# Shifted rows in two transfers, scores kept with negative sign, and other orders at the passages of a two-block kernel

## The chip, the cores and the metric

The kernel runs as one program on one core of one Trainium2 chip. The metric is the device time of one execution in microseconds (us). Before the change three runs took 1590.53 to 1592.78 us, with a median of 1591.86 us.

The core's engines each work through their own instructions in the order in which the program gives them: PE (matrix products and transposes), DVE (vector work), ACT (activations), POOL (further vector work) and SP, which here only issues transfers (DMA). Engines wait for each other through semaphores.

## The reference

The input `x` has two batches of 2048 tokens of 256 numbers. Two blocks follow, each added back to its input after a layer norm. The first block is an attention in three branches (compressed, selected, windows); the change doesn't touch it. The second has two layers of local attention and gated units, and the change lies there. Cut to that:

```python
def shift_token(t):
    t1, t2 = jnp.split(t, 2, axis=-1)
    t2 = jnp.pad(t2, ((0, 0), (1, 0), (0, 0)))[:, :-1]
    return jnp.concatenate([t1, t2], axis=-1)

def _layer(x, wqkv, qs, ksc, wo, lg, lb, w1, b1, w2, b2):
    h = shift_token(x)
    q, k, v = jnp.split(h @ wqkv, 3, axis=-1)       # 8 heads of 64
    q, k = rotary_xpos(l2norm(q) * qs, l2norm(k) * ksc)
    o = local_attention(q, k, v)                    # blocks of 128, one block back, softmax
    x = x + o @ wo
    h = shift_token(x)
    h = (h - h.mean(-1)) / jnp.sqrt(h.var(-1) + 1e-05) * lg + lb
    a, g = jnp.split(h @ w1 + b1, 2, axis=-1)       # 682 wide each
    return x + (a * jax.nn.gelu(g, approximate=False)) @ w2 + b2
```

The second half of a token's numbers thus comes from the token before it. In the attention, a query sees at most 128 keys back; other scores are masked before the softmax.

## The kernel before

**Tiles and stages.** All of `x` stays on chip: `Y[g]` holds a group of four tiles of 128 tokens, with a token's place in its tile as the partition. Groups 0 to 3 (G0 to G3) are batch 0, G4 to G7 batch 1. Up to about 240 us the first block runs (its order is the list FIRST). Then come attention of layer 0, its gated units, attention of layer 1, its gated units.

**How the order is made.** In the second block every step is a small function. `put(place, f, ...)` (line 939) files it under a place in a plan, and at the end (lines 1403 to 1405) all steps are called in order of place; each engine gets its instructions in that order. For the attention the places are those of PLACES (line 950), 12400 apart from one tile to the next (`TILE`). For the gated units they are made by `gated_units` (line 1221), one chunk every 5170 (`STEP`).

**The passages.** Where attention ends and gated units begin, and where gated units of layer 0 end and attention of layer 1 begins, steps of both are mixed. There `in_order` (line 1388) takes all steps of the stretch and puts them in the order of a list of numbers: TO_GATED (line 81, about 300 steps, used in both layers) and TO_ATTENTION (line 93, 204 steps, used once). A number is a step's rank in the plan; `w0` and `w1` are loads of later weights.

**A tile of attention.** `turn_input` transposes the tile on PE, `late_half` and `early_half` copy it to SBUF on ACT, `edge` sets the column that comes from the tile before. `project` makes queries, keys and values on PE; `square`, `sums`, `clip`, `power` and `unit` normalize on ACT, DVE and POOL; `times` and `add` rotate on DVE and POOL; `turn`, `keys` and `queries` bring queries and keys into place. `scores` multiplies them on PE. `tops` (line 1108) adds the mask to the scores with `tensor_tensor_reduce` on DVE, which also returns each row's maximum; a small DVE instruction negates the four maxima of a group of four score blocks into `off`. `exps` (line 1127) takes the exponentials on ACT with `off` as bias, `divide` divides by their sum on DVE, `turn_probs`, `probs` and `weigh` multiply with the values, `sum_first` and `sum_both` bring the result into the tile `oT`, `project_out` and `residual` add it to `Y`.

**A group of gated units.** `shift` (line 1224) makes a tile `sh`: the second halves of the group's rows, one partition further down. For that SP issues transfers: one row from the group before (`kept`), three rows from partition 127 to partition 0, and 127 rows from partitions 0 to 126 to 1 to 127. `moments` (statistics, DVE, from `Y` and `sh`), `deviations` (POOL), `normed` (DVE, eight pieces of a group) and `turned` (transposes on PE, scaling on DVE) make the input of the products. `inner` makes one chunk of gate and value on PE, `gate` does the gelu on ACT and the product on DVE (into `u`), `back` and `back_rest` multiply with `w2` on PE, `back_add` adds to `Y` on DVE, `second_bias` adds `b2` on POOL.

**Buffers.** `sh` and `oT` share one tag with two buffers. The banks of PSUM are three tags: `pa` and `pb` with two banks each, `pc` with four.

**Scores of the first block.** `win_score` (line 784) already keeps its masked scores with negative sign: scale -1, a minimum, and an exponential with scale -1.

Of the kernel before, what the change touches and what calls it, by code (L numbers as in the profile page):

```python
# [10 lines left out]
F32 = mybir.dt.float32  # L11
I32 = mybir.dt.int32
AF = mybir.ActivationFunctionType
ALU = mybir.AluOpType
AX = mybir.AxisListType

P = 128
B, L, H = 2, 2048, 256
# [18 lines left out]
FMIN = -3.4028234663852886e38  # L37
# [41 lines left out]


TO_GATED = """
39 42 140 0 1 9 18 20 22 2 5 8 11 3 17 7 4 19 24 29 47 41 14 12 15 6 13 16 10 30 33 23 40 21 26 25 34 32 36 48
38 43 54 57 51 46 67 69 35 56 61 70 89 83 64 28 31 58 71 27 45 44 50 53 37 52 63 74 77 55 87 92 59 60 66 90 76
68 73 78 91 49 97 75 62 65 85 98 79 82 84 93 96 119 72 81 80 109 123 122 101 99 103 86 121 135 94 102 120 112
118 125 127 107 126 131 129 134 113 116 115 128 88 100 105 95 110 106 114 117 104 108 139 144 111 136 143 137
150 180 167 124 133 145 149 151 141 147 158 159 132 138 155 183 185 166 170 174 152 162 165 169 130 148 142 156
160 153 161 176 146 154 164 171 173 179 178 177 184 157 191 163 172 175 186 189 198 190 194 188 195 168 w0 181
196 204 213 207 211 182 197 202 192 200 205 193 199 201 208 216 220 215 222 210 214 218 203 206 228 187 219 221
226 232 227 229 209 225 231 212 230 223 236 233 234 238 251 242 244 255 217 224 245 246 277 278 235 240 254 272
273 257 263 264 262 249 241 266 261 259 258 260 252 248 267 250 243 268 256 237 239 271 276 247 253 265 279 280  # L90
281 282 286 290 291 297 296 292 298 299 283 287 284 288 293 294 269 285 270 289 295 274 w1 275
"""
TO_ATTENTION = """
45 47 125 128 3 4 9 23 0 1 2 5 6 7 8 15 19 10 12 24 18 16 25 26 29 28 17 11 13 14 22 20 21 27 30 31 38 32 33 36
39 37 34 35 40 46 42 41 43 44 52 53 50 55 48 49 54 56 51 78 57 59 60 63 68 64 58 62 66 61 67 70 72 74 75 94 65
69 80 71 73 77 79 76 84 85 88 92 87 89 96 81 82 83 86 90 91 93 101 98 102 95 97 100 104 106 110 103 107 99 112
133 105 108 111 109 117 113 115 114 118 116 124 119 127 121 122 123 126 132 129 136 130 131 135 140 120 134 139
142 138 137 141 146 144 143 156 w0 147 145 151 150 148 149 152 153 158 154 155 160 159 157 162 165 161 166 164
163 168 172 169 167 171 174 177 181 175 173 170 182 178 183 180 179 184 185 186 191 193 187 190 189 188 195 192
200 196 202 176 201 198 199 194 197  # L100
"""


# [73 lines left out]
def sandwich_kernel(ctx: ExitStack, tc: tile.TileContext, x, Wq, bq, Wk, bk, Wv, bv, Wo, bo, Wg, bg,  # L177
                    Wc, bc, Ws, bs, wqkv, q_scale, k_scale, wo, ln_g, ln_b, w1, b1, w2, b2, rope, out):
    nc = Notes(tc.nc)
# [5 lines left out]
    small = ctx.enter_context(tc.tile_pool(name="small", bufs=6))  # L185
# [781 lines left out]
    def attention(l, base):  # L967
# [107 lines left out]
        def seen(n, half):  # L1075

            return (P - half * HALF if ORDER[n][0] == 0 else 0), KEYS
# [30 lines left out]
        def tops(n, quad):  # L1108

            s = S[n]  # L1110
            s["e", quad] = p = act.tile([P, 2, 2, KEYS], F32, tag="prob", name="prob")
            top = small.tile([P, 4], F32, tag="top4", name="top4")
            s["off", quad] = small.tile([P, 4], F32, tag="off4", name="off4")
            s["den", quad] = small.tile([P, 4], F32, tag="den4", name="den4")
            if ORDER[n][0] == 0:
                for half in range(2):
                    nc.gpsimd.memset(p[:, :, half, 0 : seen(n, half)[0]], 0.0)
            for i in range(2):
                for half in range(2):
                    lo, hi = seen(n, half)  # L1120
                    nc.vector.tensor_tensor_reduce(
                        out=p[:, i, half, lo:hi], in0=s["s", quad][half][:, i, lo:hi], in1=mask_loc[:, lo:hi],
                        scale=1.0, scalar=FMIN, op0=ALU.add, op1=ALU.max,
                        accum_out=top[:, 2 * i + half : 2 * i + half + 1])
            nc.vector.tensor_scalar_mul(s["off", quad], top, -1.0)

        def exps(n, pair):
            s = S[n]
            quad, i = divmod(pair, 2)
            for half in range(2):  # L1130
                lo, hi = seen(n, half)
                ph = s["e", quad][:, i, half, lo:hi]
                j = 2 * i + half
                nc.scalar.activation(ph, ph, AF.Exp, bias=s["off", quad][:, j : j + 1],
                                     accum_out=s["den", quad][:, j : j + 1])

        def divide(n, quad):
# [83 lines left out]
    def gated_units(l, base, no_gate_until, beside):  # L1221
        G = {g: dict(u=U[i % 2]) for i, g in enumerate(GORDER)}

        def shift(g):

            s, y = G[g], Y[g]
            sh = act.tile([P, GT, P], F32, tag="oT", name="sh")
            if g % NG:
                nc.sync.dma_start(sh[0:1, 0, :], G[g - 1]["kept"][P - 1 : P, :])
            else:  # L1230
                nc.gpsimd.memset(sh[0:1, 0, :], 0.0)
            nc.sync.dma_start(sh[0:1, 1:GT, :], y[P - 1 : P, 0 : GT - 1, P:H])
            nc.sync.dma_start(sh[1:P, :, :], y[0 : P - 1, :, P:H])
            s["kept"] = act.tile([P, P], F32, tag="kept", name="kept", bufs=3)
            nc.gpsimd.tensor_copy(s["kept"], y[:, GT - 1, P:H])
            s["sh"] = sh
# [94 lines left out]

        plan = []
        plan += [(-9, shift), (-6, deviations), (-2.5, second_bias), (-2.1, turned, 0), (-1.1, turned, 1)]
        plan += [(-7 + 0.22 * k, moments, k) for k in range(GT)]
        plan += [(-4.5 + 0.22 * (h * GT + k), normed, h, k) for h in range(2) for k in range(GT)]
# [117 lines left out]
```

## Time and profile before

The profiled execution took 1592.03 us; its span from the first to the last instruction is 1590.3 us.

| what | us |
|---|---|
| median of three runs | 1591.86 |
| profiled execution, and its span | 1592.03, 1590.3 |
| PE busy | 1507.6 (95% of the span) |
| DVE busy | 1068.6 (67%) |
| ACT busy | 758.3 (48%) |
| POOL busy | 739.2 (46%) |
| DVE waiting for the shifted rows `sh`, all places | 33.4 |
| ACT waiting for the negated maxima `off`, all places | 19.1 |

Stretches of the span, in us from its start: attention of layer 0 from about 240, the passage to gated units about 590 to 705, gated units to 880, the passage to attention of layer 1 about 880 to 970, attention to 1258, the second passage to gated units to 1370, and gated units to the end.

How to read the views. The page gives sums for the whole span. The table of stretches gives for each the busy time of PE, of PE's weight loads, of DVE, ACT and POOL, with instruction counts in brackets, and then the granted clock of PE as a share of full speed, the busy share of the DMA engines and GB/s. The chain of waits follows the work that ended last back from instruction to instruction: start, duration, what. The timeline lists instructions by start and duration, with the idle time ahead of one in square brackets and what ended it. The groups give engine, operation, output and inputs, shapes, count, then total busy us and mean ns of one, then idle time ahead. L147 is a helper through which all steps of the second block pass and L173 one for the first block, so groups are told apart by their tiles. Matrix products are pipelined, and their ends are modelled.

### The profile page before, as it was taken

The numbers are of one execution on the slowest core, as the hardware profiler recorded it, in microseconds if no ns is written. First come the engines' busy times: TensorE is split into PE (matmuls) and PEld (weight loads), VectorE is DVE, ScalarE is ACT, GpSimd is POOL, SyncE is SP. The second block draws the span as 40 slices with busy tenths as digits, with TensorE's granted clock in tenths as the row PEclk, the third lists the DMA queues.
The fourth block names the chain that finished last, engine by engine and source line by source line (L and its number), as shares of the span: only waits on it lengthen the run. The fifth ranks groups of instructions, "written<-read, shape, count | busy, mean of one in ns | idle before, by whom it ended". The sixth has DMA issues, their size and how long they took to land.

```text
span 1590.3 us, 32477 instructions
## 1 busy us (share of the span) xinstructions
PE 1507.6 (95%) x12344; PEld 983.0 (62%) x12344; DVE 1068.6 (67%) x3139; ACT 758.3 (48%) x2213; POOL 739.2 (46%) x906
## 2 busy tenths in 40 slices
PE   7999958999999999969999999999999989699998
PEld 6877743666666666535555566666666655455554
DVE  6588775787888888634445268888788885255453
ACT  4236564677677676511111157767767764011110
POOL 7214256766666666210111166666666662033233
PEclk9999979999999999989999999999999999899999
DMA  7000001100000000101000020000000000010000
GB/s 223 1 4 5 1 18 37 33 8 6 8 5 9 5 5 8 51 7 27 12 19 0 1 63 7 9 5 9 8 5 8 3 10 6 9 31 28 25 25 30
DMA packets 32510, 30.76 MB, mean 19 GB/s; under 512 B 5154, under 2 KB 30692, under 8 KB 32356
## 3 DMA queue, kind: packets, MB, share of 16 engines
q1 hardware_dynamic: 32164, 28.17, 5.9%
q8 instruction: 98, 1.61, 0.4%
q0 software_dynamic: 192, 0.52, 0.2%
q14 instruction: 56, 0.46, 0.1%
HBM read 20.30 MB, written 4.19 MB: 15 GB/s over the span
## 4 chain that ended last, share of the span: by engine, by line
PE 74%; DVE 3%; DMA 2%; POOL 2%; ACT 1%; issue 1%; SPq 0%; POOLq 0%; DVEq 0%; ACTq 0%
PE pa L147 28%; PE pb L147 24%; PE pc L147 22%; DMA sh<-Y 2%; DVE rr L147 1%; POOL rr L147 1%; DVE prob L147 1%; POOL ss L147 1%; DVE hh L147 0%; DVE Y L147 0%; ACT prob L147 0%; DVE ss L147 0%; ACT probT L147 0%; DVE u L147 0%; ACT sq L147 0%
## 5 line engine op out<-in xcount | busy, mean ns | idle before, releaser
L147 PE MATMUL pa<-wqkv,h 128*128 128x512 f32 x768 | 370.7, 606 | 15.2 <-ACT h L147 11.3
L147 POOL TENSOR_TENSOR rr<-rr 128x256 f32<-128x256 f32 x256 | 184.1, 750 | 308.0 <-DVE rr L147 252.3
L147 ACT ACTIVATE ge<-pa,vb 128x512 f32<-128x512 f32 (+1 forms) x107 | 66.7, 625 | 392.4 <-PE pa L147 324.7
L147 ACT ACTIVATE prob<-prob,off 128x192 f32<-128x192 f32 (+2 forms) x512 | 224.9, 442 | 19.7 <-DVE off L147 19.1
L147 PEld LDWEIGHTS pa<-wqkv,h 128*128 128x128 f32 x768 | 132.3, 191 | 129.1 <-issue 104.7
L147 POOL TENSOR_TENSOR ss<-ss,mhalf 128x16 f32<-128x16 f32 x64 | 187.2, 2925 | 0.8 <-DVE ss L147 0.2
L147 ACT COPY probT<-pb 128x384 f32<-128x384 f32 (+1 forms) x256 | 119.2, 469 | 120.6 <-PE pb L147 117.5
L147 PE MATMUL pa<-hh,w 128*128 128x512 f32 x368 | 171.6, 594 | 0.0
L147 PE MATMUL pb<-hh,w 128*128 128x512 f32 x292 | 141.0, 606 | 26.6 <-DVE u L147 26.6
L147 DVE CUSTOM_DVE_ANT_0 prob<-pc,mask_loc 128x192 f32<-128x192 f32 (+2 forms) x512 | 148.7, 345 | 26.0 <-PE pc L147 20.2
L147 DVE TENSOR_TENSOR rr<-pa,cs 128x1024 f32<-128x1024 f32 x128 | 151.3, 1215 | 21.5 <-ACT sq L147 19.3
L147 PE MATMUL pc<-w,u 128*128 128x256 f32 (+1 forms) x896 | 165.1, 384 | 0.0
L147 DVE SCALAR_TENSOR_TENSOR u<-pb,vb,ge 128x512 f32<-128x512 f32 x73 | 54.6, 750 | 162.3 <-PE pb L147 154.3
L147 PEld LDWEIGHTS pc<-w,u 128*128 128x128 f32 (+1 forms) x896 | 129.7, 174 | 49.0 <-issue 33.8
L147 POOL TENSOR_TENSOR rr<-rr,ss 128x512 f32<-128x512 f32 x128 | 133.1, 1059 | 2.8
L147 DVE TENSOR_TENSOR prob<-prob,den 128x768 f32<-128x768 f32 x128 | 128.1, 1001 | 4.9
L147 POOL TENSOR_SCALAR r<-mv 128x1 f32<-128x1 f32 (+1 forms) x48 | 9.2, 191 | 260.3 <-DVE mv L147 257.8
L147 PEld LDWEIGHTS pb<-ident,prob 128*128 128x128 f32 x752 | 87.9, 141 | 61.0 <-issue 31.1
L147 PE MATMUL pb<-ident,prob 128*128 128x128 f32 x752 | 118.2, 278 | 5.1 <-DVE prob L147 4.1
L147 ACT ACTIVATE sq<-pa 128x512 f32<-128x512 f32 x128 | 75.5, 592 | 98.5 <-PE pa L147 94.0
L147 PE MATMUL pb<-wo,oT 128*128 128x256 f32 x512 | 121.4, 380 | 0.2 <-DVE ss L147 0.2
L147 PEld LDWEIGHTS pb<-hh,w 128*128 128x128 f32 x292 | 56.3, 194 | 98.2 <-issue 69.5
(255 smaller groups left out, 2535.6 us busy)
## 6 DMA issues: line engine op xcount, KB each, us to landing
cs<-in_rope_dram SPq DMA_DIRECT2D x32, 128.0 KB
out_dram<-res SPq DMA_DIRECT2D x32, 128.0 KB
sh<-Y SPq DMA_DIRECT2D x16, 254.0 KB
w<-in_L_ffn_w_dram SPq DMA_DIRECT2D x6, 640.0 KB
X<-_attn_hidden_states_dram SPq DMA_DIRECT2D x7, 512.0 KB
wqkv<-in_L_ffn_wqkv_dram SPq DMA_DIRECT2D x2, 1536.0 KB
Wc<-in_L_attn_Wc_dram SPq DMA_DIRECT2D x1, 1024.0 KB
wo<-in_L_ffn_wo_dram SPq DMA_DIRECT2D x2, 512.0 KB
```

The costliest lines, as they stand in the source:

```text
L147: return f(*a, **k)
```

## The change

Three things change. The step lists TO_GATED and TO_ATTENTION hold the same steps in other orders. In `tops` the score with its mask is multiplied by -1 and its minimum is taken, so that the reduction itself gives `off`; the tile `top` and the negation go, and `exps` gets scale -1. In `shift` the transfer of 127 rows becomes two, of 112 rows (to partitions 16 to 127) and of 15 rows (to partitions 1 to 15).

```diff
@@ tops
             s["e", quad] = p = act.tile([P, 2, 2, KEYS], F32, tag="prob", name="prob")
-            top = small.tile([P, 4], F32, tag="top4", name="top4")
-            s["off", quad] = small.tile([P, 4], F32, tag="off4", name="off4")
+
+            s["off", quad] = top = small.tile([P, 4], F32, tag="top4", name="top4")
...
                     nc.vector.tensor_tensor_reduce(
                         out=p[:, i, half, lo:hi], in0=s["s", quad][half][:, i, lo:hi], in1=mask_loc[:, lo:hi],
-                        scale=1.0, scalar=FMIN, op0=ALU.add, op1=ALU.max,
+                        scale=-1.0, scalar=-FMIN, op0=ALU.add, op1=ALU.min,
                         accum_out=top[:, 2 * i + half : 2 * i + half + 1])
-            nc.vector.tensor_scalar_mul(s["off", quad], top, -1.0)
@@ exps
-                nc.scalar.activation(ph, ph, AF.Exp, bias=s["off", quad][:, j : j + 1],
+                nc.scalar.activation(ph, ph, AF.Exp, bias=s["off", quad][:, j : j + 1], scale=-1.0,
                                      accum_out=s["den", quad][:, j : j + 1])
@@ shift
             nc.sync.dma_start(sh[0:1, 1:GT, :], y[P - 1 : P, 0 : GT - 1, P:H])
-            nc.sync.dma_start(sh[1:P, :, :], y[0 : P - 1, :, P:H])
+
+            for lo, hi in ((16, P), (1, 16)):
+                nc.sync.dma_start(sh[lo:hi, :, :], y[lo - 1 : hi - 1, :, P:H])
```

The lists themselves are long; their parts that matter below, by step (a number after a tile step is the tile, counted 0 to 31 with batches alternating):

| stretch of TO_GATED in layer 0 | before | after |
|---|---|---|
| ahead of shift G4 | project_out 27 is called 35 places before it | project_out 27 is called 31 places before it, at place 197 of the list instead of 141 |
| from shift G4 to its first statistics | 36 other steps | none |
| around the end of tile 31 | probs 31 0, two normed of G4, weigh 31 | probs 31 1, turned G4 1, inner G4 1, gate G0 1, sum_both 30, probs 31 0, weigh 31 |
| around shift G1 | project_out 30, residual 30, shift G1, statistics and normed of G1, inner G4 0 to 2 with gates G4 0 to 2, sum_first 31, back G0 0 to 2, project_out 31 | inner G4 0 to 2 with gates, project_out 30, inner G0 2, gate G0 2, back G0 0 to 2, project_out 31, shift G1, statistics and normed of G1 |
| load of the next layer's wqkv | ahead of values 31 | behind shift G1 |

Behind the list both kernels go on alike: inner G4 3, gate G4 3, back G0 3, shift G5, back_rest G0, turned G1 0, inner G4 4. In TO_ATTENTION the products `back` of G3 move from ahead of the first steps of tile 0 to between them, and the load of a table (table_load 6) moves some 30 places forward.

## The prediction

> **What bounds the kernel now.** I read the page first: PE is busy 95% of a span of 1590.3 us, DVE 67%, the others under half. Only PE's idle time can be gained, so I then cut the span at the passages and read PE busy against the length of each stretch (second and third column):
>
> ```profile
> 330.00:590.00 260.00, 260.00 (x3062) 176.73 (x3053) 213.55 (x576) 182.09 (x577) 169.10 (x177) 1.00 0.02 7
> 590.00:690.00 100.00, 94.54 (x970) 58.79 (x962) 69.08 (x203) 54.64 (x164) 45.41 (x46) 1.00 0.08 25
> 690.00:705.00 15.00, 0.65 (x2) 0.33 (x2) 7.13 (x20) 0.29 (x1) 3.83 (x4) 0.66 0.03 7
> 880.00:970.00 90.00, 88.64 (x512) 52.25 (x514) 48.10 (x126) 38.15 (x116) 44.00 (x53) 1.00 0.10 29
> 1258.00:1357.00 99.00, 93.42 (x961) 58.27 (x959) 67.95 (x199) 53.67 (x160) 45.20 (x45) 1.00 0.03 8
> 1357.00:1370.00 13.00, 0.76 (x3) 0.30 (x2) 5.07 (x20) 0.26 (x1) 1.46 (x3) 0.63 0.04 9
> ```
>
> In steady attention (330 to 590) PE never idles; nothing there can gain. The passage from attention to gated units is idle 5.46 + 14.35 us in layer 0 and 5.58 + 12.24 in layer 1; the passage back (880 to 970) 1.36. The chain of waits names what fills the two long holes, and the timeline shows how:
>
> ```profile
> 680.15 16.07 DMA sh<-Y
> ...
> 1347.24 16.04 DMA sh<-Y
> ```
>
> ```profile
> 688.44 1.88 PE L147 MATMUL pa<-hh,w 128*128 128x512 f32 x4
> ...
> 696.32 0.29 DVE L147 BATCH_NORM_STATS2 st<-sh 128x6 f32<-128x128 f32 x1 [13.92 <-DMA sh<-Y]
> ...
> 704.67 3.78 PE L147 MATMUL pb<-hh,w 128*128 128x512 f32 x4 [14.35 <-DVE u L147]
> ```
>
> The rows of G1 are shifted by DMA; DVE, whose queue is in order, stands 13.92 us at their first statistics; the gates of G4 (`u`) stand behind it and hold PE's banks, so PE stops at 690.32. It restarts at half clock: four matmuls take 3.78 us there, 1.88 above, so each hole costs 1.9 us more.
>
> **The shifted rows.** Of the transfer's 16 us, the trace's packets fill 14.2: 508 of 512 bytes, one about every 28 ns. The DMA view of those 14 us and of one rope table (128 rows of 1 KB, packets within 0.9 us) shows the difference; last is the share of 16 engines:
>
> ```profile
> q1 hardware_dynamic: 509, 0.26, 7.4%
> ```
>
> ```profile
> q1 hardware_dynamic: 144, 0.13, 49.3%
> ```
>
> 7.4% of 16 is about one engine, 49.3% eight. So 127 rows went through one engine and 128 rows over many. 112 rows divide among 16 as 128 do (7 each), 127 do not; 15 rows are few either way. Bounds: no gain (one engine still: 508 packets in all) and the rope table's pace. I take the second, its row being nearest: issue to last packet 1.83 us, and 0.57 from last packet to landing, as at 695.65 to 696.22.
> The Trainium skill, "DMA: Bandwidth & Descriptors", section "Why a DMA increments its semaphore by 16 and not by 1", lets a transfer use the largest number up to 16 that divides its rows: 127 gives 1, 112 gives 16, 15 gives 15. The trace agrees for 127 and 128 rows; by it the sum below holds.
>
> Step by step: in before, the buffer came free at 678.70 and the rows landed at 696.22, 17.5 us later. Now SP issues, 0.75 us apart as before, the kept row, the three edge rows, 112 rows and 15 rows; the last starts about 2.3 us after the buffer is free and lands 2.4 later: 4.7 us. **Gain in landing: 12.8 us.** The added issue (0.7 us x 16 on SP) lies beside PE's work and is counted in the 4.7.
> With the old order, what hangs on it moves along. Layer 0: PE's restart goes from 704.67 to 691.9, its work ends at 690.32; 1.6 us of hole remain, 12.8 are gained. Layer 1: 1369.70 becomes 1356.9, before 1357.46; all 12.2 are gained. The half clock came 4.4 and 2.9 us after PE stopped and did not come in idle stretches up to 1.74 us, so it goes too: 2 x 1.9. Sum **28.8 us**. Other shifts (12 groups) lie under a full PE: 705 to 880 idles 0.5 us.
>
> **The masked scores.** 128 negations leave DVE. Priced by form:
>
> ```profile
> L147 DVE CUSTOM_DVE_ANT_0 prob<-pc,mask_loc 128x192 f32<-128x192 f32 x480 | 142.2, 351 | 16.0 <-PE pc L147 12.6 <-PE pb L147 2.4
> ...
> L147 DVE TENSOR_SCALAR off<-top 128x4 f32<-128x4 f32 x128 | 57.2, 447 | 4.4
> ...
> L173 DVE CUSTOM_DVE_ANT_0 PW<-pc,mask_win 128x96 f32<-128x96 f32 x32 | 7.5, 248 | 0.8 <-PE pc L173 0.5
> ...
> L147 DVE CUSTOM_DVE_ANT_0 prob<-pc,mask_loc 128x128 f32<-128x128 f32 x16 | 4.6, 286 | 0.0
> ...
> L147 DVE CUSTOM_DVE_ANT_0 prob<-pc,mask_loc 128x64 f32<-128x64 f32 x16 | 3.5, 220 | 10.1 <-PE pc L147 7.7 <-PE pb L147 2.4
> ```
>
> The window scores (L173) already use sign -1 and minimum: 248 ns at 96 columns, between 220 at 64 and 286 at 128, so the new form costs the same. Their exponential with scale -1 takes 369 ns at 96 columns, between 346 and 390: same. 57.2 us of DVE time go, but beside a PE that never idles; only at the first tiles (240 to 302, PE idle 8.0 us) does one negation of 0.48 us stand on the chain, at 286.21. I take **0.5 us**, bounds 0 and 2 (four of them there).
>
> **The orders.** They issue the same instructions, none more. What is left to them: 5.46 + 1.6 us, 5.58 and 1.36, 14 in all. I placed the new order beside the idle stretches. At the passage back, project 0 waited 0.86 us at 917.81 with nothing to put before it; now products of G3 (1.08 us each, ten matmuls in 2.16) stand there: gained. weigh 31 waited 0.57 us for its probabilities; now a projection of 1.72 us stands between: gained twice. turn_probs 29 waited 1.74 us for divide; now PE has both scores and two turns ahead of it, but DVE has a second times (1.23) too: not gained. At G1, the new order frees the buffer with project_out 30. From there PE holds: inner G0 2 (1.72), three products (3.24), project_out 31 (0.87), inner G4 3 (1.72), one product (1.08), the rest (about 0.9): 9.5 us, and 1.3 us within it waiting for gate G0 2. PE then meets turned G1 0, which needs 4.7 (landing) + 2.4 (statistics) + 1.3 (deviation on POOL) + 2.2 (seven short DVE pieces) = 10.6 us. 10.8 against 10.6: next late is PE itself, just. So about 1.3 us idle where the old order leaves 1.6 and 0. I take **4 us** for all orders; bounds +14 (all idle gone) and -16 (each passage as badly covered as 240 to 302, 8.0 us).
> Moved on SP: wqkv of layer 1 (issue 3.1 us, four scales 2.1) goes behind shift G1 and ahead of shift G5. G5's rows are issued 6 us later and land 13 sooner; wqkv itself is first used near 902. Cost nothing. Shift G4 is written later in the order, but SP issues it when its buffer comes free, after project_out 27; between that and its first use DVE has some 5 us of work, and the rows need about 4. The tiles sh and oT share two buffers, and a new one takes that whose last use is earliest (in before, G1 issued at 678.77, behind G4's last reader at 678.70).
>
> **Sum.** The profiled execution took 1592.03 us, 1.7 around the span, and is 0.2 above the median of the runs (1591.86), so no correction. 1592.0 - 28.8 - 0.5 - 4.0 = **1558.7**.
>
> **Rivals.**
> *The wait passes to DVE and POOL* (faster, but by half). The margin at G1 is 0.2 us. A normalization of 0.34 us took 2.37 where POOL's second bias ran beside it (701.59); two such put PE 4 us idle, which brings the half clock (1.9): 6 us per passage, and if the orders also lose their 4, 1558.7 + 16 = 1575. For it: the in-order DVE queue still holds G1's statistics ahead of gates. Against: the two biases now stand after the pieces that PE awaits. Chance 0.17.
> *The two transfers serialize* (slower). If 112 rows still go through one engine, the landing stays at 17 us, and the new order leaves shift G4 only 5 us of DVE work as cover where the old one left 17.6 (issue at 635.28, first use 652.9). DVE stands 12 us more, PE has inner G0 0, 3, 5 (4.3) as cover: 7.7 + 1.9 per passage, 1592 + 19 - 4.5 = 1607. It decides once the landing takes over some 9 us. Against it: the two DMA rows above. Chance 0.04.
> The Trainium skill, same page, section "Rules for kernel authors", advises against two transfers to disjoint halves of the partitions, since both would spread over the same engines and serialize. That presumes a transfer already spread; the 127-row one here filled 7.4%.
> *The split works, the orders lose what it gains* (no change, 1592): both passages as badly covered as the start and the half clock in each, 16 + 4, and the rival above besides. Chance 0.02; beyond it, slower, 0.01.
> *Forecast as summed*: 0.76, 1548 to 1567.
>
> **Range and chances.** Low end 1548: both transfers as summed, all 14 us of idle gone. High end 1577, which takes in the first rival. About 0.2% (3 us) can be told from no change: faster 0.93 (0.76 + 0.17), within 0.02, slower 0.05.
>
> **What would show it.** sh<-Y leaves the chain of waits, and DVE's wait for it falls from 33.4 us in all to under 5; the hole at 690 shrinks under 3 us and the granted clock there is 1.00; statistics of G1 come within 6 us of the shift; the 128x192 score stays at 351 ns. It is wrong if DVE still stands at sh for over 8 us, or if new PE idle in 590 to 705 exceeds 10 us.

## The result, and the profile after

| kernel | median, us | runs | ratio to before, 95% interval |
|---|---|---|---|
| before | 1592.32 | 1590.53 to 1593.54 (4) | |
| after | 1569.12 | 1561.26 to 1569.64 (4) | 0.9843 (0.9819 to 0.9868) |

The change saves 23 us, 1.6%; 1558.7 was predicted, with a range of 1548 to 1577. The profiled execution of after took 1569.13 us, its span is 1567.4. PE's idle time up to its last product fell from 75.1 to 52.6 us and its busy time stayed (1507.6 and 1507.2). One of the four executions, at 1561.26, stands apart from the other three, at 1569.10 to 1569.64; the experiments below look at what separates such groups.

Four stretches of after, in the table of stretches (length; then PE, its weight loads, DVE, ACT, POOL; granted clock, DMA share, GB/s). Layer 1 comes 13 us earlier than in before, so its window is moved:

```profile
590.00:690.00 100.00, 92.17 (x948) 58.74 (x949) 68.81 (x183) 52.14 (x156) 44.31 (x43) 0.97 0.03 7
690.00:705.00 15.00, 14.95 (x58) 10.73 (x57) 7.10 (x24) 0.69 (x1) 1.80 (x4) 1.00 0.09 21
880.00:970.00 90.00, 88.94 (x664) 55.45 (x667) 51.70 (x140) 45.12 (x139) 52.49 (x62) 1.00 0.10 31
1244.00:1345.00 101.00, 93.08 (x950) 58.95 (x949) 70.35 (x189) 53.58 (x163) 45.13 (x44) 0.97 0.03 7
```

From 690 to 705, where PE stood 14.35 us, it now works 14.95 of 15 at full clock. But ahead of it, from 590 to 690, 7.83 us are idle where before had 5.46, and the mean clock is 0.97 where it was 1.00. Layer 1 repeats this. So the long hole went and a new loss came earlier.

The timeline of after (start, duration, what; idle time in brackets) shows the new hole:

```profile
628.99 1.20 DVE L147 TENSOR_SCALAR hh<-Y,mv,r 128x128 f32<-128x128 f32 x1
629.06 1.04 POOL L147 TENSOR_TENSOR rr<-rr,ss 128x512 f32<-128x512 f32 x1
630.06 1.41 POOL L147 TENSOR_TENSOR rr<-rr 128x256 f32<-128x256 f32 x2
630.11 2.56 DVE L147 TENSOR_SCALAR hh<-sh,mv,r 128x128 f32<-128x128 f32 x3
631.54 1.04 POOL L147 TENSOR_TENSOR rr<-rr,ss 128x512 f32<-128x512 f32 x1
632.59 0.59 DVE L147 TENSOR_SCALAR hh<-Y,mv,r 128x128 f32<-128x128 f32 x2
632.82 0.58 ACT L147 COPY oT<-pc 128x512 f32<-128x512 f32 x1 [4.04 <-POOL rr L147]
633.44 0.69 DVE L147 TENSOR_TENSOR oT<-oT,pc 128x512 f32<-128x512 f32 x1 [0.26 <-ACT oT L147]
634.18 2.53 PE L147 MATMUL pb<-wo,oT 128*128 128x256 f32 x8 [2.23 <-DVE oT L147]
```

Read it from the bottom. PE waits 2.23 us to project the output of tile 28 (`project_out`), because DVE makes `oT` (`sum_both`) only at 633.44. Ahead of that in DVE's queue stand eight normalizations of G0 (`normed`). They took 627.63 to 633.18, 5.5 us, where eight at the pace of the two from 632.59 (0.3 each) would take 2.4. The six long ones stand beside POOL's rotations and unit scales (`rr`), and each of the six ends 0.08 to 0.09 us after a POOL operation does: the one of 628.99 at 630.19, POOL's at 630.10; the last of the three of 630.11 at 632.67, POOL's last at 632.58. The Trainium skill, "SBUF — State Buffer", section "Who interferes with whom", says that some VectorE operations and GpSimd's share one pair of ports as an exclusive lock, so that the later one stands until the other is done. The trace agrees in these ends. But not every instruction of POOL slows them. In split_sign, a run described below, the same pieces of G0 run beside one that makes `ss`, at their usual 0.34 us each:

```profile
627.06 2.89 POOL L147 TENSOR_TENSOR ss<-ss,mhalf 128x16 f32<-128x16 f32 x1
627.37 0.60 DVE L147 TENSOR_SCALAR hh<-sh,mv,r 128x128 f32<-128x128 f32 x2
```

So the trace shows the slowing beside `rr` and not beside `ss`; no run here takes `rr` away from the eight. That their pace, and not only their place, makes the sum late is worked out: 5.5 less 2.4 is 3.1 us, more than the hole.

ACT's copy (`sum_first`), at 632.82, waits besides: its `oT` takes the buffer of the shifted rows of G0, which the last of those normalizations on `sh` reads. The label "POOL rr" on its wait is the last event by the profile and not the cause: the copy doesn't read `rr`, and that normalization ends at 632.67 (with a third buffer, below, the copy doesn't wait for it).

The same hole stands at 1287.40 to 1289.63, and after each of the two the clock is halved for 6.83 us (from 635.50 and from 1290.86).

The groups by form, for the masked scores and their exponentials:

```profile
L147 ACT ACTIVATE prob<-prob,top 128x192 f32<-128x192 f32 x480 | 213.3, 448 | 9.8 <-DVE top L147 9.8
L147 DVE CUSTOM_DVE_ANT_0 prob<-pc,mask_loc 128x192 f32<-128x192 f32 x480 | 142.4, 353 | 55.4 <-PE pc L147 43.9 <-PE pb L147 11.5
```

A score takes 353 ns (351 before); the negations' group is gone; ACT waits 9.8 us for the maxima where it waited 19.1 for `off`. The waits list has no row any more in which DVE waits for `sh` (33.4 us before).

### The profile page after: what moved, and what is told of

It reads as the page before. It is cut to its first block, busy times and chain, and to the rows that moved or that the text cites. A ratio compares the mean times of both kernels' runs of the same rounds, so it can differ in the third digit from the quotient of the medians.

```text
span 1567.4 us, 32418 instructions
## 1 busy us (share of the span) xinstructions
PE 1507.2 (96%) x12344; PEld 985.7 (63%) x12344; DVE 1020.8 (65%) x3011; ACT 756.9 (48%) x2213; POOL 740.1 (47%) x906
## 4 chain that ended last, share of the span: by engine, by line
PE 74%; DVE 4%; ACT 2%; issue 1%; POOL 1%; POOLq 0%; ACTq 0%; DVEq 0%
PE pa L147 28%; PE pb L147 24%; PE pc L147 22%; DVE prob L147 1%; ACT prob L147 1%; POOL rr L147 1%; DVE hh L147 1%; DVE rr L147 1%; DVE u L147 0%; DVE Y L147 0%; POOL r L147 0%; ACT ge L147 0%; DVE oT L147 0%; ACT sq L147 0%; POOL ss L147 0%
## 5 line engine op out<-in xcount | busy, mean ns | idle before, releaser
L147 ACT ACTIVATE prob<-prob,top 128x192 f32<-128x192 f32 (+2 forms) x512 | 224.9, 443 | 9.9 <-DVE top L147 9.8
L147 PE MATMUL pb<-hh,w 128*128 128x512 f32 x292 | 137.2, 592 | 0.0
L147 PE MATMUL pc<-kr,qT 64*64 64x192 f32 (+2 forms) x2688 | 111.4, 293 | 6.3 <-ACT qT L147 4.3
```

Source lines behind the costliest of these rows:

```text
L147: return f(*a, **k)
```

## The experiments

The theory at the start: the split gives what was predicted or more, the new orders take back, through the hole at tile 28 and the half clock that follows. The rival: the split or the sign gives less in this company, and the orders are neutral. The three parts were first run each alone.

### The transfer split alone: 112 and 15 rows, and 113 and 14

```diff
 # split_only: the list orders and the scores of before
-            nc.sync.dma_start(sh[1:P, :, :], y[0 : P - 1, :, P:H])
+            for lo, hi in ((16, P), (1, 16)):
+                nc.sync.dma_start(sh[lo:hi, :, :], y[lo - 1 : hi - 1, :, P:H])
 # split_113_14: the same with
+            for lo, hi in ((15, P), (1, 15)):
```

> The kernel before with the 127 shifted rows sent as 112 and 15, nothing else changed. If the row count decides how many engines a transfer takes, the rows of G1 land 4 to 5 us after their buffer is free instead of 17.5, the two PE holes at 690 and 1357 shrink from 14.35 and 12.24 us to under 2, no half clock follows them, and the time falls by some 28.8 us to about 1563. If two transfers share one path one after the other, landing stays near 17 us and the time at 1592.

> The kernel before with the 127 rows sent as 113 and 14. Also two transfers of nearly the same sizes, but 113 has no divisor up to 16. If divisibility of the row count is the cause, the 452 packets of the first transfer still go through one engine, landing stays at 14 to 16 us and the time at 1587 to 1594. If any cut into two is enough, or if the long rows only have to be fewer, it falls to about 1563 as with 112 and 15.

| kernel | median, us | ratio, 95% |
|---|---|---|
| 112 + 15 rows | 1562.88 (1560.98 to 1563.59) | 0.9815 (0.9802 to 0.9829) |
| 113 + 14 rows | 1591.18 (1589.46 to 1592.27) | 0.9993 (0.9984 to 1.0003) |

Both were run beside a before of 1592.41. Two transfers in place of one are worth 29.5 us with one cut and nothing that can be told with the other, one row away. The DMA view of each, GB/s in 40 slices, first 112 + 15 from 678 to 685 us (slices of 0.175 us):

```profile
GB/s 0 0 0 0 94 0 0 0 0 0 0 0 0 3 1 0 0 6 3 0 0 0 184 219 219 252 234 167 158 47 6 0 0 0 0 0 0 0 0 0
```

Then 113 + 14 from 678 to 696 us (slices of 0.45 us):

```profile
GB/s 36 0 0 0 1 0 3 1 16 9 14 13 23 22 22 19 19 19 18 19 19 18 19 18 19 19 18 19 19 18 35 62 19 19 18 19 2 0 0 0
```

158 to 252 GB/s for 1.2 us against 18 to 23 in most slices of some 12 us. In the trace's packets, the 508 packets of the 112 and 15 rows have ended 2.78 us after the issue of the first of the two transfers. The 452 packets of the 113 rows follow each other, one about every 28 ns as in before, as through one DMA engine, and the last ends 14.1 us after their issue. The 14 rows beside them, to partitions 1 to 14, pass in 0.4 us (691.84 to 692.24, with up to 13 packets under way at a time). So it isn't the odd first partition that keeps a transfer on one engine. The timelines of the two, in the same order:

```profile
679.75 2.43 SPq L147 DMA_DIRECT2D sh<-Y  x3
683.71 0.29 DVE L147 BATCH_NORM_STATS2 st<-sh 128x6 f32<-128x128 f32 x1 [0.98 <-DMA sh<-Y]
692.07 1.98 PE L147 MATMUL pb<-hh,w 128*128 128x512 f32 x4 [1.41 <-DVE u L147]
```

```profile
694.98 0.29 DVE L147 BATCH_NORM_STATS2 st<-sh 128x6 f32<-128x128 f32 x1 [12.60 <-DMA sh<-Y]
703.33 2.07 PE L147 MATMUL pb<-hh,w 128*128 128x512 f32 x2 [13.04 <-DVE u L147]
```

DVE waits 0.98 us for the rows against 12.60, PE 1.41 against 13.04. So the row count decides and not the number of transfers. By the rule that the prediction drew on in the Trainium skill, "DMA: Bandwidth & Descriptors", section "Why a DMA increments its semaphore by 16 and not by 1", 113 rows get one engine like 127, and the trace agrees. By the Trainium skill's advice against two transfers to disjoint halves of the partitions (same page, section "Rules for kernel authors"), the 29.5 us would have been left.

### The sign alone, and with the split

```diff
 # sign_only; split_sign has the split of 112 + 15 too
...
-                        scale=1.0, scalar=FMIN, op0=ALU.add, op1=ALU.max,
+                        scale=-1.0, scalar=-FMIN, op0=ALU.add, op1=ALU.min,
...
-            nc.vector.tensor_scalar_mul(s["off", quad], top, -1.0)
...
-                nc.scalar.activation(ph, ph, AF.Exp, bias=s["off", quad][:, j : j + 1],
+                nc.scalar.activation(ph, ph, AF.Exp, bias=s["off", quad][:, j : j + 1], scale=-1.0,
```

> The kernel before with negative scores alone: 128 fewer instructions on DVE, 57 us of its busy time. If they lie beside a full PE, the time falls by 0.5 us (0 to 2), that is 1591.5. If DVE's queue limits any passage, the idle stretches of PE between 600 and 690 shrink too and it falls by 2 to 4 us.

> The kernel before with 112 and 15 rows and with negative scores, old step lists. If parts add up, it is 1562.9 less 0.5 to 1.4, that is 1561.5 to 1562.4, which is faster than the full change's usual 1569: the new lists then cost up to 7 us. If the lists gain, this is slower than the changed kernel's best, 1561.3.

The sign alone gave 1591.0 us (1590.1 to 1593.07), ratio 0.9995 (0.9986 to 1.0004): 1.4 by the medians, not to be told from nothing. Its profile has one half-clock stretch that before's has not (3.41 us from 256.16) and a longer one at G1 (17.07 us for 13.65), so a part of what it saves may be lost to the clock. With the split it gave 1560.84 (1559.34 to 1561.62), ratio 0.9803 (0.979 to 0.9816): 2.0 under the split alone by the medians, which were not timed side by side, and a little below the 1561.5 to 1562.4 that were expected. The table of stretches has part of it, at the first tiles, in split_only and then in split_sign:

```profile
290.00:302.00 12.00, 11.55 (x93) 6.98 (x84) 9.35 (x28) 7.95 (x28) 9.16 (x10) 1.00 0.30 85
```

```profile
290.00:302.00 12.00, 12.00 (x114) 7.81 (x114) 9.29 (x27) 8.82 (x28) 8.76 (x10) 1.00 0.28 81
```

A hole of 0.45 us (at 296.94) is gone. Ahead of it, from the first score of a group to the reciprocal of its sums, DVE takes 3.98 us in split_only (285.20 to 289.18), with two negations of 0.47 and 0.36 us between, and 3.36 in split_sign (284.68 to 288.04). Counted by PE's starts, the lead of split_sign over split_only grows by 1.27 us between 290 and 330, and that of sign_only over before by 1.28. The part of it that is no idle time isn't explained by a run here.

### The orders alone

```diff
 # orders_only: both lists of the change, transfer and scores of before
-TO_GATED, TO_ATTENTION: lists of before
+TO_GATED, TO_ATTENTION: lists of the change
```

> The kernel before with the new step lists alone, 127 rows still in one transfer. If the lists are made for fast rows, DVE stands at the first statistics of G4 for 8 to 12 us and again at G1, and the time is above before: 1600 to 1612 (1607 by the prediction's rival plus the negations). If the lists gain by themselves, it is 1580 to 1590.

1596.35 us (1593.71 to 1597.4, 9 runs), ratio 1.0024 (1.0014 to 1.0034): slower by 4 us, in neither of the two ranges that were expected. Its waits list has one row for the rows' wait (total, times, longest):

```profile
DVE st L147 <- DMA sh<-Y: 39.7, 5, 13.3
```

and its timeline shows what that costs at G1:

```profile
714.54 0.29 DVE L147 BATCH_NORM_STATS2 st<-sh 128x6 f32<-128x128 f32 x1 [13.27 <-DMA sh<-Y]
721.54 1.11 PE L147 MATMUL pc<-ident,hh 128*128 128x128 f32 x4 [6.78 <-DVE Y L147]
```

With rows that still take 17 us, the new order covers G1 better (6.78 us of PE's idle time, where the old order had 14.35) and pays at G4 (2.39 at 668.62) and at tile 28 (2.35 at 634.08). PE is idle 73.8 us in all, hardly under the 75.1 of before, but its busy time is 3.0 us longer: after 250 us it works at half clock in three places. The prediction's slow rival had priced this company (new orders, slow rows) at 1607, 15 us over before, because it put the loss at G4 on top of an unchanged hole at G1. The orders lose here by 4.

### After once more: two groups of times in one kernel

> The changed kernel, unaltered, more executions. If its 6 to 8 us above 1561 come from half-clock stretches that the idle time at project_out 28 sets off in some executions, the executions fall into two or three groups, near 1561 with a mean granted clock of 0.993, near 1569 with 0.987, and perhaps one between, with the clock telling which. If the orders simply cost that much, all lie within 2 us of one value whatever the clock.

The kernel after, run again, unchanged, gave 1563.19, 1563.88, 1569.72, 1564.59 and 1562.82 us, ratio 0.9831 (0.9814 to 0.9847). Of all nine executions four took 1569 to 1570 and five 1561 to 1565. The mean granted clock goes with it in eight: 0.987 in the four, 0.991 to 0.993 in four of the five. The ninth, 1564.59, has 0.987 too and is short all the same; it has no profile, and why stays open. The profile taken this time is one of the short ones. It has the same hole, 2.25 us at 633.26 and 2.24 at 1285.18, and no half clock after it. Both spans can be laid on each other: PE's instructions in the long one come 1.3 us earlier at 250 us, then fall behind by 3.5 us in the first passage and 3.7 in the second; over the whole span PE is busy 4.8 us longer and idle 1.2 longer.

Why does the same hole halve the clock once and not the other time? In all profiles the half-clock stretches begin and end on a grid of 3.413 us that runs through the execution. Here are the cells of the grid around the hole. First after, with the half clock behind it:

```profile
632.09:635.50 3.41, 1.32 (x6) 1.19 (x7) 3.15 (x13) 1.56 (x3) 0.50 (x1) 1.00 0.00 0
635.50:642.33 6.83, 6.16 (x74) 4.73 (x73) 6.01 (x9) 2.34 (x9) 3.36 (x3) 0.50 0.01 2
```

Then after_again, without:

```profile
630.75:634.16 3.41, 2.51 (x20) 1.20 (x11) 3.41 (x5) 0.01 (x1) 3.08 (x4) 1.00 0.01 2
634.16:637.58 3.42, 2.07 (x11) 1.82 (x12) 3.16 (x12) 1.55 (x3) 0.00 (x0) 1.00 0.00 0
```

In the first, one cell holds nearly the whole hole: PE busy 1.32, idle 2.09 of 3.41. In the second the hole straddles a border, 0.90 us of idle time on one side and 1.35 on the other. That the place of the grid relative to the program parts the times is inferred from these profiles; no run sets it, and the execution of 1564.59 doesn't fit without more.

### Is it the place of one step? project_out of tile 28 later

```diff
 # po28_later: after, in TO_GATED two steps behind project 31 2
-... 153 157 177 184 118 148 156 161 176 164 160 163 191 168 172 ...
+... 153 157 118 148 156 161 176 164 160 163 191 168 177 184 172 ...
```

> The changed kernel with project_out 28 and residual 28 moved behind project 31 2 in TO_GATED, so that PE has turn 30, scores 30 and project 31 2 to do while sum_both 28 is late. If the 2.23 us hole at 632 and 1287 sets off the half clock, both the hole and the half clock go, no execution shows 0.987, and the time is 1558 to 1562. If the half clock has another source (the sum of small idle stretches in the passage, 7.7 us), it stays and the time is 1565 to 1569.

1569.41 us (1567.86 to 1569.89), ratio 0.9854 (0.9839 to 0.9869): no gain, with the clock at 0.991 or 0.992 in all four executions. Neither of the two cases that were expected came: hole and half clock are gone, and the time is that of the long executions. PE doesn't wait for `oT` any more, and waits for others, 1.63 us at 636.28 for `qT` among them:

```profile
642.86 0.42 DVE L147 TENSOR_TENSOR Y<-pb,Y 128x256 f32<-128x256 f32 x1 [2.67 <-PE pb L147]
644.51 0.84 PE L147 MATMUL pb<-ident,prob 128*128 128x128 f32 x6 [1.69 <-DVE den L147]
```

The idle time grew to 57.0 us in all, 5.5 more than in after_again. The wait for `qT` still comes from the eight: ACT's copy into `oT` runs only at 634.17, after the last normalization on `sh` (634.02), and `qT` stands behind it in ACT's queue. The wait for `den` comes from the edit itself: `residual` 28 was moved along, stands ahead of `den` in DVE's queue, and holds DVE 2.67 us for the projection that now comes later. So to move these two steps hands the wait on and adds one; how far the place alone counts, this run can't say.

### The eight normalizations out of the way; a third buffer

```diff
 # cover: after; in TO_GATED five of the eight normed of G0 (1 0, 1 1, 1 2, 0 3, 0 1)
 # go behind clip 31, and the tag has three buffers
-... 143 180 152 162 167 174 159 149 115 ... 173 179 123 ...
+... 143 180 152 115 ... 173 179 162 167 174 159 149 123 ...
-            S[n]["oT"] = act.tile([P, HEADS // 2, P], F32, tag="oT", name="oT")
+            S[n]["oT"] = act.tile([P, HEADS // 2, P], F32, tag="oT", name="oT", bufs=3)
...
-            sh = act.tile([P, GT, P], F32, tag="oT", name="sh")
+            sh = act.tile([P, GT, P], F32, tag="oT", name="sh", bufs=3)
 # after_oT3: the third buffer alone
```

> The changed kernel with three buffers for sh and oT, and five of the eight normed of G0 moved behind clip 31 in TO_GATED, so that sum_first 28 need not wait for the last reader of sh and sum_both 28 stands behind three normed only. It removes the cause instead of covering it. If the shared buffer and the normed ahead in DVE's queue make project_out 28 late, its 2.23 us hole falls under 0.5, no half clock follows, and the time is 1557 to 1562. If the slow pieces of DVE beside POOL only move on, another hole of 1 to 2 us appears behind it and the time stays between 1562 and 1569.

> The changed kernel with three buffers for sh and oT and the step lists as they are. sum_first 28 then needs not wait for the last reader of sh. If the eight normed ahead of sum_both 28 in DVE's queue are what is late, the hole only shrinks by some 0.3 us to 2.0, and the time stays at 1563 or, with the half clock, 1569. If the shared buffer was the cause, the hole falls under 1 us and the time to 1560 as in the run with both edits.

cover: 1559.94 us (1558.76 to 1560.49), ratio 0.9798 (0.9785 to 0.9812), 3.9 under the median of after_again, timed beside it. Its timeline:

```profile
630.63 0.69 DVE L147 TENSOR_TENSOR oT<-oT,pc 128x512 f32<-128x512 f32 x1
632.15 1.89 PE L147 MATMUL pb<-wo,oT 128*128 128x256 f32 x8
633.88 0.86 DVE L147 TENSOR_SCALAR hh<-sh,mv,r 128x128 f32<-128x128 f32 x3
```

Three normalizations stay ahead of `sum_both`, the sum is there at 631.32, PE doesn't wait, and the moved ones, now behind POOL's rotations and scales, run at 0.29 us each.

after_oT3: 1561.28 us (1560.58 to 1562.08), ratio 0.9806 (0.9791 to 0.9821). With a buffer of its own the copy on ACT runs at 629.87 and not at 632.82, but the sum on DVE stays behind the eight at 633.33, and the hole shrinks only from 2.25 to 1.88 us. So the queue of normalizations is the cause and the shared buffer 0.37 us of it. The mean clock is 0.991 or 0.992 in all four executions, and the profile has no half clock in the passages. The hole came out as expected, the time 1.7 us below the 1563 that went with it.

### A longer hole on purpose

```diff
 # hole_longer: after, with a sum nobody reads ahead of sum_both of tile 28
+            if n == 28:
+                nc.vector.tensor_reduce(small.tile([P, 2 * HEADS], F32, tag="ss", name="ss"), ..., AX.X, ALU.add)
```

> The changed kernel with one more DVE instruction (a sum over 128x1024, 1.2 us, its result unused) ahead of sum_both 28 in each layer, so that the hole at project_out 28 grows from 2.25 to about 3.4 us. If the length of this hole sets off the half clock, it comes in every execution and in both layers (granted clock 0.987), and the time is 1563.5 + 2.4 + 7 = 1573. If it comes by chance and not from the hole, some executions stay at 0.991 and 1566.

1566.3 us (1565.17 to 1569.89), ratio 0.984 (0.9827 to 0.9854). The hole came out at 3.01 us. The half clock was expected in every execution and in both layers; that failed. The mean clock was 0.990, 0.987, 0.990, 0.989 and 0.990. The profile has it in layer 1 alone. In each layer the cell of the grid that holds most of the hole, layer 0 first:

```profile
634.82:638.23 3.41, 1.58 (x7) 1.43 (x8) 3.41 (x12) 1.25 (x3) 0.00 (x0) 1.00 0.00 0
1286.76:1290.17 3.41, 0.90 (x4) 0.82 (x5) 3.41 (x12) 1.56 (x3) 0.14 (x1) 1.00 0.00 0
```

In layer 0 PE is idle 1.18 us of the cell before and 1.83 of this one, and keeps its clock; in layer 1 it is idle 2.51 of one cell, and the clock is halved from 1290.17. So here the idle time within a cell counts and not the length of the hole: this run speaks against the theory that a longer hole always costs the clock, and for the grid.

### Which list, and the best of all

```diff
 # split_sign_att: split, sign and the new TO_ATTENTION; TO_GATED of before
 # old_list_oT3: the same, and bufs=3 in the two places of cover
```

> The kernel before with 112 and 15 rows, negative scores and the new TO_ATTENTION, but the old TO_GATED. If the cost of the orders lies in TO_GATED, this is 1560.8 less at most 0.5, the idle time that the passage back lost. If TO_ATTENTION costs, it is above 1562.

> The kernel before with 112 and 15 rows, negative scores, the new TO_ATTENTION, the old TO_GATED, and three buffers for sh and oT. If the last reader of G4's shifted rows is what holds back the transfer for G1, a third buffer lets SP issue it some 25 us earlier, DVE never stands at its statistics, the 1.47 us hole at 689 goes, and the time is 1559, as low as the run with the moved normed. If DVE's own eight normed and POOL beside them set that hole, it stays at 1.0 us or more and the time at 1560.5.

split_sign_att took 1560.61 us (1558.84 to 1560.99), ratio 0.9798 (0.9785 to 0.9812); split_sign, without the new TO_ATTENTION, had 0.9803. That list does nothing that can be told; after differs from this run in TO_GATED alone, so the cost of the orders lies there. old_list_oT3 took 1559.41 us (1558.36 to 1559.72), ratio 0.9793 (0.9779 to 0.9806), the lowest median of all, though cover's interval overlaps. With the old list and a third buffer, SP need not wait for G4's last reader to shift G1:

```profile
649.25 0.60 SPq L147 DMA_DIRECT2D sh<-kept  x1
```

```profile
689.13 1.98 PE L147 MATMUL pb<-hh,w 128*128 128x512 f32 x4 [0.35 <-DVE u L147]
```

In split_only it issued at 679.10, 30 us later, and PE's wait at this place was 1.41 us (1.47 in split_sign_att).

## Why the prediction was right, and where it was wrong

The forecast was faster and the time lies in its range, 10.4 us over the number. It lies above 1548 to 1567, the range of the forecast as summed, and inside the stated range only because that was widened to 1577 for the first rival. That after_again's median, 1563.88, lies in the narrower range too is luck: in both the orders' term has the wrong sign. By its own terms:

| term | predicted, us | measured, us |
|---|---|---|
| split, with the half clock | -28.8 | -29.5 (split_only against before) |
| sign | -0.5, bounds 0 and -2 | -1.4 alone (not to be told from nothing), -2.0 on the split |
| orders | -4, bounds -14 and +16 | +3.0 (1563.88 of after_again against 1560.84 of split_sign), +8.3 with the half clock (1569.12) |

**The split** went as worked out, in its parts too: between the profiles of before and split_only, PE's idle time falls by 24.9 us (12.8 + 12.2 summed) and its busy time by 4.1 (3.8 summed). The rows of G1 were said to land 4.7 us after the buffer is free; in split_only it is 4.7 from the last reader's end to the first statistics on them (679.03 to 683.71), where before took 17.6 (678.70 to 696.32). The remaining hole was put at 1.6 in layer 0 and is 1.41. Layer 1 has none, as said. With the old order the half clock went from the passages too: split_only's profile has none between 250 and 1550 us. The row count was the cause, as 113 + 14 shows, and the rival in which the two transfers serialize is out.

**The sign** was under-sized by about 1 us. The single negation on the chain at 286.21 was taken; the one behind it, at 287.91 in before, counts too, as the 0.62 us on DVE show (3.98 against 3.36, more than one negation of 0.47), and the upper bound of 2 just held what came. The score's price (351, now 353 ns) and the exponential's held.

**The orders** are the step that failed, in size and sign: "what is left to them" was read from the old idle stretches one by one, each asked whether the new order fills it. The 4 us aren't the sum of the answers either: 0.86 + 2 x 0.57 gained, 0.3 gained at G1 in layer 0 and 1.3 lost in layer 1 make 1.0, and no row stands behind the rest. Two answers hold. weigh 31's 0.57 us is gone. At G1 PE works 14.95 of 15 us, where 10.8 us of work were set against 10.6 needed. Two fail: project 0's 0.86 us at the passage back, called gained, still stands at 904.16 (0.86); turn_probs 29's 1.74 us, called not gained, is gone (from 590 to 705 no transpose of probabilities waits over 0.30 us). What the new order makes late that was not late before was asked at G1 and for shift G4, and not at tile 28. The eight normalizations of G0 now stand in a row ahead of tile 28's sums; in split_sign they lie among tile 28's other work (627 to 633.4), and PE's projections there have no wait. With the rows fast in both, the whole passage of layer 0 idles 6.86 us with the old order (split_sign, 590 to 692) and 7.89 with the new (after, 590 to 705). And with that hole taken away the new lists still gain nothing that can be told: cover took 1559.94 us, the old list with the same third buffer 1559.41. So the gain that was forecast isn't there, and the hole with its half clock makes the loss.

**The mechanism was on record as a rival**, "The wait passes to DVE and POOL": normalizations slowed beside POOL's work, PE a few us idle, then the half clock. It was put at G1 beside the second bias, priced at 6 us per passage and given 0.17. It came at tile 28 with POOL's rotations. So the kind of loss was foreseen and its place was not. The sums differ as well: 1575 was the rival's time, 1569 and 1563 came.

**The half clock** was called gone on the ground that idle stretches up to 1.74 us hadn't brought it. That held for the old list and not for the hole of 2.23. That a stretch of this length brings it in some executions and not in others could not be read from before, which has none between 1.75 and 12 us in its passages.

Of the signs that were named: `sh` out of DVE's waits, under 3 us at the old hole with a clock of 1.00, statistics within 6 us of the shift (696.66 in after, for a shift issued from 691.72), the score at 351 (353), all came. "New PE idle in 590 to 705 over 10 us" did not: it is 7.9 in all (7.83 + 0.05).

## What to carry to other kernels

Count the rows of a transfer before counting its bytes: where the trace shows packets one after another on one engine, cut it so that the large part divides among the engines, and check with a cut one row off. When a long wait is gone, a list that was ordered around it has to be judged anew by every queue that it touches: ask of each in-order engine what now stands ahead of the next thing PE needs, and what runs beside it on the engine that slows it. And the idle time within any 3.4 us is best kept under 1.6 us: no cell that began at full clock brought the half clock here with less. With a hole a little over 2 us a kernel can have two groups of times, and a few runs show either.

## What the runs showed of the hardware that was not expected

The clock of PE falls on a grid. In the fourteen profiles (before, after, and the twelve runs) the half-clock stretches last 3.41, 6.83, 13.65, 17.07, 20.48 or 23.89 us and start at multiples of 3.413 us from each other, all through an execution; only the last one's length, which the end of the execution cuts, does not fit. PE's idle time counted within each cell at full clock after 250 us parts them: every such cell with 2.03 us or more of idle time was followed by half clock, none with 1.75 or less, and between (1.76 to 1.83 us) both occur. In the first block, before 250 us, one cell with 1.64 us was followed by it too (after, from 215.66), so the bound isn't the same for all work of PE. The Trainium skill, "TensorE: Matmul & The Clock Gate", section "What's actually happening", gives such a free-running window of 3413 ns, with which the lengths agree, and puts the drop after at least one idle window. These cells were not idle: PE worked 1.32 of 3.41 us in the one before 635.50 and 0.90 in the one before 1290.17, and the clock was halved behind both. The measurement decides: in the passages here the bound lies between 1.75 and 2.03 us of idle time in a cell.

One such drop of 6.83 us costs about 3 us: after and after_again differ by 5.94 us in their profiled executions (1569.13 and 1563.19) with two drops between them, and PE works 6.16 of the 6.83 us at half speed. Why a drop lasts one cell in hole_longer (3.41 us) and two in after isn't explained here.
